# A shared centre tap between even and odd pixels in a Winograd-row convolution, with named buffers, a masked group norm and a re-planned order, on one Trainium2 core

## The chip, the core and the metric

The kernel runs on one core of one Trainium2 chip. The metric is device time in microseconds (us): the median of several runs of the same program. All tensors are float32, and TensorE takes each float32 matmul as two passes.

## The reference

The input x is (4 images, 128 channels, 128 x 128 pixels). Two layers follow, each with a residual.

```python
# layer 0
x = x + L0(group_norm(x))
# L0: block(v) + block(v transposed in space) transposed back, equal here to 2 * block(v)
# block, per pixel ("token") over 128 channels:
t = ln(t); y1 = ln(t)
t = t + (sigmoid(y1) * y1) @ W_out.T
y2 = ln(t); wht = y2 @ W_whiten.T
k = relu(wht @ W_key.T) ** 2                  # 512 wide
t = t + sigmoid(wht @ W_recep.T) * (k @ W_value.T)
# layer 1
x = x + L1(group_norm(x))
# L1: a 3x3 convolution (128 to 128 channels, padding 1) plus bias, times a squeeze-excite gate per channel
```

group_norm has 32 groups of 4 channels. The convolution needs the statistics of the whole image after layer 0, so an image is convolved only when its first layer is finished.

## The kernel before, in words

*Tiling.* Channels lie on the 128 partitions. An image is 32 chunks of 512 pixels (CH); two chunks make a group g (16 groups an image, 64 in all), and 16 image rows make a block k (8 an image, 32 in all), which is four chunks.

*Layer 0* (`layer0(g)`). For both chunks h of a group: the input is normalised on ScalarE (`u`, L757), turned to tokens-on-partitions on VectorE (`ut`, L886), has its statistics taken (`bn0`, L770), is scaled on ScalarE (`t`, L839) and multiplied and shifted by the norm's parameters (`g`, `b`, L908 and L911, on GpSimd from group 2 on). Second norm (`bn1`, `z`), back to channels (by TensorE, `Tz` L942, or from group 22 on by DMA through `zd`, `zs`, `zc`), silu, the attention product (`att`, L954), the residual (`T`, L959), third norm (`bn2`, whose factor goes through `four`, `rrow`, `rd`, `R`). t goes back to channels by DMA too (`td` L850, `ts`, `tt`). `cp` (L1015) makes y2. Then four key products `pk` (L1033), a relu each on ScalarE (L1038), a square each (on ScalarE L1044, or on VectorE L1050, as the table `SQUARES` says), the receptance `pr` (L1058), four value products `kv` (L1071) that accumulate into one bank, the gate step `q` (L1080) that reads that bank, the residual add on GpSimd (`x1`, L1086) and the statistics of the result (`bx`, L1094). A finished block is stored to DRAM (`xo`, L1101).

*Layer 1* (`conv(k, at)`). Rows are combined so that six products give four output rows (a Winograd transform along the rows): VectorE makes v1, v2, v3, v4, v0, v5 (L1179 to L1193) from rows of the block; TensorE makes m_i from v_i (`product`); VectorE and ScalarE combine the m_i into four rows (L1218 to L1239), and the block is stored (L1249). Each v_i and m_i is 128 x 512: four rows of 128 pixels. A product is three matmuls into one bank, one for each tap along the row; the outer taps leave out one column at the edge of the image:

```python
nc.tensor.matmul(pc, u[:, 1], vv, start=True, stop=False)
nc.tensor.matmul(pc[:, :, 1:W], u[:, 0], vv[:, :, 0 : W - 1], start=False, stop=False)
nc.tensor.matmul(pc[:, :, 0 : W - 1], u[:, 2], vv[:, :, 1:W], start=False, stop=True)
```

*Weights.* `conv_setup(b, at)` makes the second group norm and the gate of image b (`cag`, `cpm`, `csp`, ... `csg`) and scales the six transformed weights uw (`us` L621, `ut2` L627). `input_norm(b, at)` makes the first group norm of image b: the channel means of `bn_aggr` are averaged over the four channels of a group by one-column matmuls on TensorE (L498, L500), the variances by more of them, then GpSimd takes the root.

*What sets the order.* Nothing is left to the hardware's choice. `Plan` records every step with its engine, an assumed cost, a priority (its group, plus an entry of the table `SHIFT`), what it reads and writes and what buffers it takes; `Plan.order` lists the steps by simulated start on five in-order engines (TensorE, VectorE, ScalarE, GpSimd, and SyncE, whose queue issues the DMAs), and the kernel emits the instructions in that order. `ROOM` says how many buffers each kind has, also the eight PSUM banks: 3 of `Bh` (pk, pr, small products), 1 of `Bkv`, 2 of `Btr` (att and the TensorE transposes), 2 of `Bconv` (m_i). Buffers of a kind are taken in rotation. The convolution of image b is given priorities from group 16(b+1)+2 on, two groups apart for each block, so that it runs beside layer 0 of image b+1; the last image's convolution has nothing beside it. While the head of the kernel has gaps on TensorE, matmuls of no use (`fill`, L411) keep it going.

Of the kernel before, what the change touches and what calls it, by code (L numbers as in the profile page):

```python
# [13 lines left out]
P = 128  # L14
# [9 lines left out]
    "R": -94.694, "Rc": 15.085, "Rm": -2.646, "S": 24.009, "T": -84.8, "Tz": -36.19, "W": -22.14,  # L24
    "ab": 37.315, "att": 1.644, "b": 31.731, "bn0": 11.794, "bn1": -17.35, "bn2": -15.592,
    "bx": 49.609, "c": 7.82, "cag": 6.719, "cav": -18.068, "cd": -103.804, "cp": -37.768,
    "cp1": -27.368, "cpm": -17.233, "cpr": -71.755, "cpv": -65.194, "cre": 48.407, "crt": -73.005,
    "csg": -26.086, "csp": -39.311, "cth": -29.247, "cve": 53.942, "e": 12.136, "e0": 14.7,
    "e1": -70.81, "e2": -55.971, "edge": 60.492, "fw": 14.887, "g": -16.106, "gag": -13.379,
    "gnb": -14.148, "gpm": -2.701, "gpv": -23.531, "grt": -1.635, "gsp": -6.989, "gve": -30.013,  # L30
    "hot": -13.329, "in": 26.361, "in0": 105.375, "kv": 3.816, "late": 12.753, "m0": 23.5,
    "m1": -101.213, "o": -54.585, "pk": 3.497, "pq": -18.954, "pr": 3.288, "q": -106.007,
    "raw": -61.508, "rc": -6.337, "re": -93.796, "silu": -97.676, "sq": -115.033, "sqd": -34.912,
    "t": -2.49, "tD": -49.255, "tR": 16.588, "tW": -20.948, "th": -60.823, "tt": 105.266,
    "u": 16.271, "us": -19.465, "ut": 67.807, "ut2": 9.337, "uw": -50.513, "v": 57.985, "w": 117.982,
    "w0": 44.736, "w1": -43.048, "w2": -6.943, "x": 70.181, "x1": -70.076, "xc": 6.78, "xd": 2.407,
    "xf": -58.371, "xo": -10.863, "xs": -54.606, "y": 24.867, "z": 15.121, "zD": 21.243,
    "zR": 18.813, "zW": -13.966,
}
SQUARES = (("DDAA", "DDAA"), ("AAAA", "AAAA"))  # L40
# [3 lines left out]
LOOK = {'PE': 0.018, 'DVE': 0.087, 'ACT': 0.048, 'POOL': 0.004, 'SP': 0.048}  # L44
HASTE = 31.975
SQUARES_AT = 17
ROOM = dict(
    x=3, xd=2, xs=2, ut=3, t=7, z=2, y=2, zd=2, zc=2, td=2, tt=2, R=2, y2=2, h=6, r=2, xc=2, vt=3, v=4,
# [3 lines left out]
BACKLOG = 1.96  # L52
FIRST_U_ON_DVE = (2, 3)


XF_BUS, FIRST_XD, LATE_AT = 3.4, -25, -5
FILL_UNTIL, FILL_STEP = 330, 1.2
FIRST_FILL = {6: 3, 7: 2}
# [29 lines left out]

class Plan:
# [11 lines left out]
    def op(self, name, eng, cost, prio, emit, reads=(), writes=(), new=(), port=False, bus=0.0):  # L101
# [13 lines left out]
        for u in (*reads, *writes):  # L115
            if u[0] in self.users:
# [3 lines left out]
                 new=[t for t, _ in new], port=port, bus=bus)  # L120
# [3 lines left out]
    def order(self):  # L124
# [14 lines left out]
        freed, queue, taken = {}, {}, {}  # L139
# [12 lines left out]
        def slots(o):  # L152
            at = 0.0
            count = {}
            for t in o["new"]:
                tag = self.home[t]
                k = taken.get(tag, 0) + count.get(tag, 0)
                count[tag] = count.get(tag, 0) + 1
                if k >= self.room[tag]:
                    old = queue[tag][k - self.room[tag]] if k - self.room[tag] < len(queue[tag]) else None  # L160
                    if old is None or pending[old]:
                        return INF
                    at = max(at, freed[old])
            return at

        while done < n:
# [54 lines left out]
            for t in o["new"]:  # L221
                tag = self.home[t]
                queue.setdefault(tag, []).append(t)
                taken[tag] = taken.get(tag, 0) + 1
            for t in touches[i]:
                pending[t] -= 1
                freed[t] = max(freed.get(t, 0.0), en)
            for j in after[i]:
                reach = (self.OWN if ops[j]["eng"] == e else self.REACH)[ops[j]["eng"]]
                ready[j] = max(ready[j], en + reach)  # L230
                left[j] -= 1
                if not left[j]:
                    waiting[ops[j]["eng"]].append(j)
# [9 lines left out]
def conv_preact_kernel(  # L243
# [42 lines left out]
        z=[P, SUB, C], y=[P, CH], y2=[P, CH], h=[P, CH], r=[P, CH],  # L286
        xc=[P, BLK_ROWS + 2, W], vt=[P, Q, W], v=[P, Q, W], yt=[P, Q, W], uw=[P, 3, P],
# [9 lines left out]
    def make(t, tag):  # L297
        pool = ps if tag[0] == "B" else sb
        T[t] = pool.tile(SHAPE[tag], F32, tag=tag, name=t[0], bufs=ROOM[tag])
        return T[t]  # L300

    def bank(name):
        return ps.tile([P, CH], F32, tag="Bh", name=name, bufs=ROOM["Bh"])

    def staged(name, n, src=None):
        t = sb.tile([P, n], F32, tag="h", name=name, bufs=ROOM["h"])
# [4 lines left out]
    vec = sb.tile([5, C], F32, tag="vt", name="vec", bufs=ROOM["vt"])  # L311
# [3 lines left out]
    for name, src in (("g0row", ln0_g), ("b0row", ln0_b)):  # L315
        row0.append(sb.tile([1, C], F32, tag="y2", name=name, bufs=ROOM["y2"]))
# [3 lines left out]
    wo = sb.tile([P, P], F32, tag="v", name="wo", bufs=ROOM["v"])  # L320
# [26 lines left out]
    gmat = gmat.rearrange("p a b -> p (a b)")  # L347
    gturn = const.tile([P, SUB, P], F32, tag="gturn", name="gturn")
    for q in range(SUB):
# [3 lines left out]
        )  # L353

# [10 lines left out]
    ones = sb.tile([1, P], F32, tag="r", name="ones", bufs=ROOM["r"])  # L365
    nc.gpsimd.memset(ones, 1.0)

    warm = sb.tile([P, 1], F32, tag="r", name="warm", bufs=ROOM["r"])
# [38 lines left out]
    fill = ps.tile([P, CH], F32, tag="Bconv", name="fill", bufs=ROOM["Bconv"])  # L407
# [14 lines left out]
    READ, WRITE = (0, 0.85), (0, 0.4)  # L422

    def op(name, eng, cost, prio, emit, reads=(), writes=(), new=(), port=False, bus=0.0):
        return plan.op(name, eng, cost, prio + SHIFT.get(name, 0.0), emit, reads, writes, new, port, bus)
# [58 lines left out]
    def input_norm(b, at):  # L484
# [5 lines left out]

        def aggregate():
            S["mv"] = col("mv0", 2)
            nc.vector.bn_aggr(S["mv"], st0.pop(b).rearrange("p n s -> p (n s)"))

        def grouped(key, src, own):
            pm = T[key]
            for q in range(SUB):
                nc.tensor.matmul(pm[:, q : q + 1], gturn[:, q], src, start=True, stop=True)  # L498
            if own:
                nc.tensor.matmul(pm[:, SUB : SUB + 1], gmat, src, start=True, stop=True)  # L500

        def means():
            make(("pm0", b), "Bh")
            grouped(("pm0", b), S["mv"][:, 0:1], True)

        def spread():
# [5 lines left out]
            S["q"] = q  # L512

        def variances():
            make(("pv0", b), "Bh")
            grouped(("pv0", b), S["q"], False)
# [13 lines left out]
        step("gag", V, (0.4, 0.5), aggregate, [(s, i) for i in range(NCH)], [(("gnv", b), 0)])  # L530
        step("gpm", E, (0.5, 0.55), means, (), [(("pm0", b), 0)], [(("pm0", b), "Bh")])
        step("gsp", V, (0.65, 0.75), spread, [(("pm0", b), 0)])
        step("gpv", E, (0.4, 0.45), variances, (), [(("pv0", b), 0)], [(("pv0", b), "Bh")])
# [4 lines left out]
    def conv_setup(b, at):  # L538
# [7 lines left out]
        def small(name, eng, cost, fn, bank=None):  # L546
            t = (name, b)
            step(name, eng, cost, fn, (), [(t, 0)] if bank else (), [(t, "Bh")] if bank else ())
# [58 lines left out]
        small("csp", V, (0.8, 0.9), spread)  # L607
        small("cpv", E, (0.1, 0.15), variances, True)
        small("cve", V, TINY, with_eps)
# [3 lines left out]
        small("cre", V, (0.2, 0.3), rect)  # L613
        small("cpr", E, (0.3, 0.35), second, True)
        small("cth", A, (0.6, 0.75), tanh)
# [13 lines left out]
        for i in (1, 2, 3, 4, 0, 5):  # L629
# [10 lines left out]
            )  # L640
            if i in TAP:
                op("ut2", V, (0.21, 0.29), at, lambda i=i: tapped(i), [(t, 0)], [(t, 0)], (), True)

# [677 lines left out]
```

## Time and profile before

| what | us |
|---|---|
| median of 3 runs | 1744.41 (1743.2 to 1745.63) |
| the profiled execution | 1742.63 |
| its span, first to last instruction | 1740.9 |
| first key product (pk) starts | 71.1 |
| products of the convolution of images 0, 1, 2, 3 begin | 428.9, 850.0, 1301.5, 1612.4 |
| last value product (kv) | 1578.2 |
| last matmul | 1736.4 |
| m products on PE (L1203, L1204, L1205) | 197.7 + 195.4 + 194.9 busy |

A line of instruction groups gives the line of the kernel, engine, operation, tiles out<-in, shapes and count, then the busy time in us and the mean duration in ns, then the engine's idle time just before them and what ended it. A busy time is a union, so overlapping matmuls count once, and the durations of matmuls are longer than the spacing of their starts, since they are pipelined. PEld is TensorE's weight load. The granted TensorE clock was 0.997 on average.

### The profile page before, as it was taken

To read this page: it belongs to the slowest core of one execution; us is meant where nothing else is said; L and a number is where in the kernel's file an instruction comes from. 1 tells how busy PE (TensorE), PEld (TensorE's weight loads), DVE (VectorE), ACT (ScalarE), POOL (GpSimd) and SP (SyncE) were. 2 spreads that over 40 slices of the span, in tenths; PEclk is the share of its full clock that TensorE was granted. 3 is DMA by queue.
4 is the path that set the end of the run, shared out by engine and by line. 5 is a ranking of instruction groups with operands and counts; after the bars stand their busy time and mean duration, and the time that the engine had idled before them with its cause. 6 is when DMAs were issued, how large, how long until landed. Compare 5 with 4: busy or idle time off the path is not lost.

```text
span 1740.9 us, 18709 instructions
## 1 busy us (share of the span) xinstructions
PE 1690.7 (97%) x4872; PEld 815.7 (47%) x4872; DVE 1424.9 (82%) x2619; ACT 1293.8 (74%) x2656; POOL 1184.0 (68%) x1085
## 2 busy tenths in 40 slices
PE   5899999999999999999999999999999999999999
PEld 2444544444444445444445445454544444444443
DVE  5898888788889967798998887888897766448986
ACT  1999998898988887889889877998887875440000
POOL 1778887788987885879777886988878773310000
PEclk9999999999999999999999999999999999999999
DMA  9366675466577777578778877577776565215321
GB/s 326 91 213 202 193 219 194 145 206 230 153 250 246 252 230 236 199 232 247 250 245 245 254 238 240 178 218 236 241 254 199 183 204 176 101 75 224 154 98 73
DMA packets 140170, 354.66 MB, mean 204 GB/s; under 512 B 19079, under 2 KB 78750, under 8 KB 122782
## 3 DMA queue, kind: packets, MB, share of 16 engines
q1 hardware_dynamic: 139472, 352.99, 63.1%
q8 instruction: 39, 0.64, 0.2%
q14 instruction: 69, 0.57, 0.1%
q10 hardware_dynamic: 590, 0.46, 0.1%
HBM read 230.31 MB, written 123.07 MB: 203 GB/s over the span
## 4 chain that ended last, share of the span: by engine, by line
PE 71%; ACT 10%; POOL 8%; DVE 7%; DMA 2%; issue 2%; SPq 0%; ACTq 0%; DVEq 0%; POOLq 0%
PE kv L1071 19%; PE pk L1033 18%; PE m L1203 7%; PE m L1204 7%; PE m L1205 7%; PE att L954 5%; PE pr L1058 5%; ACT t L839 2%; ACT h L1038 2%; POOL rs L820 2%; ACT z L839 2%; DVE st L770 1%; ACT h L1044 1%; POOL x L1026 1%; POOL t L908 1%
## 5 line engine op out<-in xcount | busy, mean ns | idle before, releaser
L1071 PE MATMUL kv<-h,wv 128*128 128x512 f32 x1024 | 525.8, 598 | 4.6 <-DVE r L1080 2.6
L1033 PE MATMUL pk<-y,wk_s 128*128 128x512 f32 x1024 | 480.9, 595 | 4.7 <-ACT h L1038 3.1
L1038 ACT ACTIVATE h<-pk,kbias 128x512 f32<-128x512 f32 x512 | 336.1, 682 | 90.9 <-PE pk L1033 88.3
L1033 PEld LDWEIGHTS pk<-y,wk_s 128*128 128x128 f32 x1024 | 190.0, 190 | 239.3 <-issue 178.1
L1071 PEld LDWEIGHTS kv<-h,wv 128*128 128x128 f32 x1024 | 183.0, 190 | 205.3 <-issue 164.1
L1044 ACT ACTIVATE h<-h 128x512 f32<-128x512 f32 x444 | 267.5, 629 | 2.6
L1086 POOL TENSOR_TENSOR x<-x,r 128x512 f32<-128x512 f32 x128 | 169.8, 1327 | 132.0 <-DVE r L1080 128.5
L820 POOL TENSOR_TENSOR rs<-rs,nhalf 128x8 f32<-128x8 f32 (+1 forms) x134 | 227.2, 1700 | 47.3 <-ACT rs L817 45.1
L839 ACT ACTIVATE z<-t,nb,rs 128x128 f32<-128x128 f32 x512 | 208.7, 489 | 21.8 <-POOL nb L825 20.9
L839 ACT ACTIVATE t<-ut,nb,rs 128x128 f32<-128x128 f32 x512 | 209.7, 488 | 8.5 <-POOL nb L825 4.8
L908 POOL TENSOR_TENSOR t<-t,g 128x512 f32<-128x512 f32 x124 | 161.2, 1301 | 68.0 <-ACT t L839 67.6
L770 DVE BATCH_NORM_STATS2 st<-t 128x6 f32<-128x256 f32 x512 | 187.1, 410 | 22.9 <-POOL t L911 22.7
L1203 PE MATMUL m<-v,uw 128*128 128x512 f32 x384 | 197.7, 596 | 3.9 <-DVE v L1182 3.9
L1204 PE MATMUL m<-v,uw 128*128 128x508 f32 x384 | 195.4, 590 | 0.0
L1205 PE MATMUL m<-v,uw 128*128 128x508 f32 x384 | 194.9, 589 | 0.0
L1015 POOL TENSOR_TENSOR y<-tt,R 128x512 f32<-128x512 f32 x96 | 130.9, 1367 | 59.8 <-PE pk L1033 46.9
L1026 POOL TENSOR_TENSOR x<-tt,x 128x512 f32<-128x512 f32 x124 | 162.5, 1324 | 3.9 <-DMA tt<-ts 3.7
L911 POOL TENSOR_TENSOR t<-t,b 128x512 f32<-128x512 f32 x124 | 162.7, 1319 | 2.6
L954 PEld LDWEIGHTS att<-wo,y 128*128 128x128 f32 x1024 | 130.9, 192 | 51.7 <-issue 33.1
L1063 ACT ACTIVATE r<-pr,rbias 128x512 f32<-128x512 f32 x128 | 87.1, 681 | 72.6 <-PE pr L1058 36.2
L1058 PE MATMUL pr<-y,wr_s 128*128 128x512 f32 x256 | 132.3, 600 | 3.9 <-ACT h L1038 3.0
L954 PE MATMUL att<-wo,y 128*128 128x128 f32 x1024 | 132.8, 276 | 0.4 <-ACT y L947 0.3
(160 smaller groups left out, 2278.6 us busy)
## 6 DMA issues: line engine op xcount, KB each, us to landing
xd<-in_x SPq DMA_DIRECT2D x128, 256.0 KB
x<-in_x SPq DMA_DIRECT2D x32, 1024.0 KB
xo<-x SPq DMA_DIRECT2D x32, 1024.0 KB
R<-rd SPq DMA_DIRECT2D x63, 512.0 KB
ts<-td SPq DMA_DIRECT2D x248, 128.0 KB
tt<-ts SPq DMA_DIRECT2D x62, 512.0 KB
out<-xc SPq DMA_DIRECT2D x31, 1024.0 KB
xc<-xo SPq DMA_DIRECT2D x24, 1152.0 KB
```

Of the source, the lines that this page charges most:

```text
L770: nc.vector.bn_stats(st[:, i : i + 2, :].rearrange("p n f -> p (n f)"), two)
L820: nc.gpsimd.tensor_tensor(T[rs][:, part], T[rs][:, part], nhalf[:, :k], ALU.pow)
L839: nc.scalar.activation(dst[:, s, :], src[:, s, :], AF.Identity, bias=nb[:, i : i + 1], scale=rs[:, i : i + 1])
L954: nc.tensor.matmul(pa[:, ts(m, P)], T[y][:, ts(m, P)], wo2, start=True, stop=True)
L1033: nc.tensor.matmul(make(pk, "Bh"), wk_s[:, ts(j, P)], T[y2], start=True, stop=True)
L1038: nc.scalar.activation(make(hh, "h"), T[pk], AF.Relu, bias=kbias[:, j : j + 1])
L1044: nc.scalar.activation(T[hh], T[hh], AF.Square)
L1058: nc.tensor.matmul(make(pr, "Bh"), wr_s, T[y2], start=True, stop=True)
L1071: nc.tensor.matmul(T[kv], wv[:, j, :], T["h", g, h, j], start=(j == 0), stop=(j == NH - 1))
L1203: nc.tensor.matmul(pc, u[:, 1], vv, start=True, stop=False)
L1204: nc.tensor.matmul(pc[:, :, 1:W], u[:, 0], vv[:, :, 0 : W - 1], start=False, stop=False)
L1205: nc.tensor.matmul(pc[:, :, 0 : W - 1], u[:, 2], vv[:, :, 1:W], start=False, stop=True)
```

## The change

1. *Shared centre tap.* For blocks k < 24 (images 0 to 2) the products 1, 3, 0 and 5 are made otherwise (`PARITY`). v_i is written as two runs, the even pixels of the rows and the odd ones. With taps a, c, b (left, centre, right) and pair k of even and odd pixels e and o, the even output pixel is c(e[k] + o[k]) + (b - c)o[k] + a o[k-1], and the odd one c(e[k] + o[k]) + (a - c)e[k] + b e[k+1]: both hold the centre tap of the sum. VectorE makes that sum (`su`, 256 columns) and once an image the differences of outer and centre taps (`ud`); TensorE makes four products of 256, 252, 256 and 252 columns into the bank of m_i and one shared product of 256 columns (`cm`) into a bank of `Btr`; VectorE adds the shared bank to what is made of m_i (`cs`, 512 columns).
2. *Squares.* The tile h holds two chunks' worth of hidden units (1024 columns), three of them in place of six; most squares are taken on ScalarE over 1024 columns at once ("W").
3. *Buffers.* A buffer of a kind is taken by name, whichever was freed first, and not in rotation. `zd` and `td` have one buffer each, where they had two.
4. *Masked first norm.* Means and variances are multiplied by a 0/1 mask (`own`) on VectorE, and one matmul of four columns with `gany` takes the place of four of one column.
5. *Order.* All entries of `SHIFT` and other planner settings are new; the first four groups have entries for each half (`lag`). The planner also knows of four waits in `conv_setup` that it left out before. The fill matmuls on the input in the head (`FIRST_FILL`) are gone.

Products 2 and 4, and all six in image 3, keep their three matmuls. The core of the diff:

```diff
-SQUARES = (("DDAA", "DDAA"), ("AAAA", "AAAA"))
+SQUARES = (("DAWW", "DDWW"), ("WWWW", "WWWW"))
+SUM_BANK = "Btr"
...
-    x=3, xd=2, xs=2, ut=3, t=7, z=2, y=2, zd=2, zc=2, td=2, tt=2, R=2, y2=2, h=6, r=2, xc=2, vt=3, v=4,
+    s=2, ud=4,
+    x=3, xd=2, xs=2, ut=3, t=7, z=2, y=2, zd=1, zc=2, td=1, tt=2, R=2, y2=2, h=3, r=2, xc=2, vt=3, v=4,
...
-FIRST_FILL = {6: 3, 7: 2}
+FIRST_FILL = {}
...
+def PARITY(k):
+    return (0, 1, 3, 5) if k < 24 else ()
...
-        T[t] = pool.tile(SHAPE[tag], F32, tag=tag, name=t[0], bufs=ROOM[tag])
+        T[t] = pool.tile(SHAPE[tag], F32, tag=f"{tag}-{plan.slot[t]}", name=t[0], bufs=1)
...
+        def split(name, src):
+            S[name] = col(name, SUB)
+            nc.vector.tensor_scalar(S[name], own, src, None, ALU.mult)
...
-            grouped(("pm0", b), S["mv"][:, 0:1], True)
+            nc.tensor.matmul(pm[:, :SUB], gany, S["m4"], start=True, stop=True)
+            nc.tensor.matmul(pm[:, SUB : SUB + 1], gmat, S["mv"][:, 0:1], start=True, stop=True)
...
+                    nc.vector.tensor_tensor(make(ud, "ud"), u[:, 0::2], u[:, 1:2].to_broadcast([P, 2, P]), ALU.subtract)
...
+                elif how == "W" and not first:
+                    def square(hh=hh):
+                        x = T[hh].rearrange("p a b -> p (a b)")
+                        nc.scalar.activation(x, x, AF.Square)
...
+                def both(i=i, su=su):
+                    x = flat_halves(i)
+                    dst = make(su, "s").rearrange("p (q k) -> p q k", q=Q)
+                    nc.vector.tensor_tensor(dst, x[:, 0], x[:, 1], ALU.add)
...
+                    nc.tensor.matmul(pc[:, 0], d[:, 1], x[:, 1], start=True, stop=False)
+                    nc.tensor.matmul(pc[:, 0, :, 1:], u[:, 0], x[:, 1, :, : W // 2 - 1], start=False, stop=True)
+                    nc.tensor.matmul(pc[:, 1], d[:, 0], x[:, 0], start=True, stop=False)
+                    nc.tensor.matmul(pc[:, 1, :, : W // 2 - 1], u[:, 2], x[:, 0, :, 1:], start=False, stop=True)
...
+                    nc.tensor.matmul(make(mm, SUM_BANK)[:, : CH // 2], T["uw", b, i][:, 1], T[su], start=True, stop=True)
...
+                t = by_parity(get(n))
+                row = T[name_of(f"mm{i}")][:, : CH // 2].rearrange("p (q k o) -> p q k o", q=Q, o=1)
+                tt(t, row.to_broadcast([P, Q, W // 2, 2]), t, ALU.add)
```

## The prediction

> **What bounds the kernel now.** I read the page's totals and its chain of waits first, then the busy time of each engine in stretches of the span, then who TensorE waits for, then single matmuls in time order.
>
> ```profile
> PE 1690.7 (97%) x4872; PEld 815.7 (47%) x4872; DVE 1424.9 (82%) x2619; ACT 1293.8 (74%) x2656; POOL 1184.0 (68%) x1085
> ...
> PE 71%; ACT 10%; POOL 8%; DVE 7%; DMA 2%; issue 2%; SPq 0%; ACTq 0%; DVEq 0%; POOLq 0%
> ```
>
> A busy PE need not be a full one, so the stretches decide (length, then the busy time of PE, PEld, DVE, ACT, POOL):
>
> ```profile
> 0.00:80.00 80.00, 53.70 (x181) 29.71 (x182) 55.11 (x111) 43.05 (x105) 33.40 (x63) 0.98 0.70 220
> 80.00:330.00 250.00, 239.86 (x790) 120.86 (x789) 214.10 (x414) 229.53 (x479) 201.35 (x192) 0.99 0.62 196
> 330.00:600.00 270.00, 266.13 (x799) 129.96 (x798) 238.39 (x454) 236.10 (x496) 228.67 (x208) 1.00 0.69 214
> 600.00:1370.00 770.00, 767.85 (x2199) 370.09 (x2198) 650.62 (x1192) 657.71 (x1342) 626.23 (x548) 1.00 0.73 230
> ...
> 1580.00:1612.00 32.00, 28.49 (x74) 12.57 (x72) 29.80 (x61) 2.09 (x5) 1.47 (x2) 1.00 0.70 271
> 1612.00:1741.00 129.00, 124.63 (x288) 55.21 (x288) 106.76 (x175) 10.20 (x16) 0.00 (x0) 0.99 0.28 110
> ```
>
> From 600 to 1370 us PE lacks 2.2 us in 770. DVE is busy for 650.6, 84.5% of it. The waits of PE in that stretch name almost nothing:
>
> ```profile
> PE kv L1071 <- DVE r L1080: 0.9, 2, 0.8
> PE cpv L565 <- DVE q L561: 0.5, 1, 0.5
> PE pr L1058 <- POOL y L1015: 0.5, 1, 0.5
> PE pk L1033 <- ACT h L1038: 0.2, 1, 0.2
> ```
>
> Are the matmuls back to back? The timeline gives starts, and each x2 is the two passes of one fp32 matmul:
>
> ```profile
> 704.45 1.02 PE L1203 MATMUL m<-v,uw 128*128 128x512 f32 x2
> 705.31 1.01 PE L1204 MATMUL m<-v,uw 128*128 128x508 f32 x2
> 706.16 1.01 PE L1205 MATMUL m<-v,uw 128*128 128x508 f32 x2
> 707.01 1.02 PE L1071 MATMUL kv<-h,wv 128*128 128x512 f32 x2
> ...
> 784.66 1.02 PE L1071 MATMUL kv<-h,wv 128*128 128x512 f32 x2
> 785.52 1.05 PE L954 MATMUL att<-wo,y 128*128 128x128 f32 x8
> ```
>
> A product of three matmuls starts at 704.45 and its successor at 707.01: 2.56 us. The steady spacing in the trace is 0.4295 us a pass for 512 columns, 0.426 for 508 and 0.1115 for 128 (0.112 for one column). So the convolution costs TensorE its columns, and while images 0 to 2 are convolved beside the next image's first layer, every column taken away is time.
>
> **The products: minus 40.0 us.** Four of six products (1, 3, 0, 5) in 24 of 32 blocks change: 96 of 192. Before, two passes each of 512, 508 and 508 columns: 2 x (0.4295 + 2 x 0.426) = 2.563 us. After, two passes each of 256, 252, 256, 252 and the shared 256. No 256-column row exists. Half of the 512 row gives 0.2148 us, the line between the 128 and 512 rows 0.2175; I take 0.216 (0.2125 for 252): 2 x (3 x 0.216 + 2 x 0.2125) = 2.146. Saved 0.417 each, x96 = 40.0 us; the two ends give 41.1 and 38.5.
>
> One rule would cancel this. The Trainium skill, "TensorE: Matmul & The Clock Gate", section "The mechanism", lets a weight load overlap running matmuls only in another row group, and "LDWEIGHTS (loading the stationary operand)" prices 128 columns at about 107 ns. All these matmuls use all rows. With loads exposed, ten passes in place of six would add 4 x 0.107 = 0.43 us and turn the saving into a loss of about 1 us over 96 products. The rows say otherwise: a 512-column pass with its own load takes 0.4295 us, and a 128-column pass, again with its own load, 0.1115: little more than the page gives the load alone. At 256 columns there is twice that room. I stay with 40.0.
>
> **The masked first norm: minus 5.0 us.** Each image's group means took 18 one-column passes and now take 6 (two of four columns and one of one): 12 x 0.112 = 1.34 us. For images 1 to 3 this lies on the full PE, 4.0 us; in the head it is on the chain before the first image, where two masking steps on DVE (0.16 each, as L520) come in: 1.0 us net.
>
> **The order in the head: 0, between -8 and +8.** In the built order of before, pr, four pk and four kv of group 0 (0.86 + 3.4 + 3.4 us) stand among the groups' att and transposes and have run by 80 us. In the order of after all these att and transposes come first, then nine fill matmuls (7.7 us of warming), then the first pk. That can cost the 7.7 us. What it feeds is a stretch (80 to 330) that lost 10.1 us on PE, with ACT at 92%. With a stock of finished inputs some of these come back. I put it at nought. ACT stays as tight there: squares become 51 on DVE (68 before), 17 single and 222 double on ACT (444 single before).
>
> **What is added, all on DVE: plus 84 us of work, of which I charge 12.** In 96 products a sum of the two halves (256 elements; nearest row L770, 256 elements, 0.33 us start to start) and an addition of the shared bank (512, one PSUM input, nearest L1222 to L1239, 0.60 to 0.63 from start to start where DVE doesn't idle): 96 x 0.94 = 90. Twelve tap differences at 0.33 = 4, eight masks 1, less 17 squares at 0.67 = 11. Sum 84. The strided forms read two runs in turn; L770 reads its two rows the same way at full rate, so I add nothing for the stride (0 to 5 us).
>
> It fits beside PE only just. From the gate product of group 24 to that of group 56, before takes 768 us (601 to 1369). Counting instructions in the built orders at the rates above, PE has 754 us before and 772 after (18 blocks of products there, 15 before), DVE 578 and 686. Measured, DVE was busy 649, a factor 1.12. In the dense piece 487 to 601 us DVE was busy 104.5 of 114.2 us for a counted 97.7, a factor 1.07, and PE still 113.0. So after: DVE 733 (1.07) to 769 (1.12) in a stretch where PE needs 772. The factor is mostly this (DVE busy of L1189, first with GpSimd working, then with it idle):
>
> ```profile
> 600.00:1370.00 770.00, 15.45 (x14) 1.00 0.73 230
> 1612.00:1741.00 129.00, 5.46 (x8) 0.99 0.28 110
> ```
>
> 1.10 us against 0.68: a DVE step with two SBUF inputs waits for a GpSimd step. The half sums and the tap differences are of that kind (up to 0.2 us more each, 108 x 0.2 = 22 of the 84 us again); the additions of the shared bank, one input in PSUM, are not. Behind a late DVE stand the gate step (frees the only kv bank, the next kv waits in PE's queue), t plus att, and v. At 91% busy (487 to 601) PE lost 1.2 us in 114, 1%; at 95% I take 1.5% of 772 us. Cover all gone: 30 us or more.
>
> **Edits at nought.** Double squares on ACT: 222 start later than single ones by one relu (0.57 us by L1038), hidden by other PE work, since PE's queue mixes pk and kv of different groups; at the last group, where nothing else is left to mix in, it costs one such relu at most. Buffers named by who is free first: no instruction. td and zd with one buffer: the transposes at 703.3 are written by transfers issued from 704.0 to 710.7 and fetched at 714.2, and the next come about 24 us later (768 / 32); if that failed, DVE's queue would stop behind the transpose, 0 to 5 us. The shared product uses the two banks of att and the transposes; att waits in PE's queue if both are held, 0 to 5 us. Stage change to image 3: 13.5 us of products are left behind the last kv in place of 28.2, but the chain from there to image 3's first product was itself held up by those products; its PE stall was about 5 us (28.5 busy of 32, and slower matmuls for a moment after it) and I leave it.
>
> **Sum.** 1740.9 (span) - 40.0 - 5.0 + 0 + 12 = 1707.9. The profiled execution took 1742.6 and the median is 1744.4, 3.5 over the span: 1711.
>
> **Rivals.** (1) *DVE shares the bound*: 733 becomes 769 and PE stalls 4 to 5% in the conv stretches: 15 to 25 us more, 1726 to 1736, middle 1730. For it: 84.5% plus 84 us; against: only 2.2 us of stall now, and 91% did no harm. (2) *DVE is the bound, slower*: half sums at L1189's hindered price (0.53), factor 1.12 and a DVE that cannot be over 94% busy because it too waits: 769 / 0.94 = 818 us for the stretch, 46 over PE's 772. It gives back the whole 45 saved, with some in the stretch before: 1750. It decides from a DVE share of about 97% of PE's need. (3) *The weight loads are not hidden at 256 columns*: no gain from products, 1711 + 41 = 1752; the 128-column row excludes nearly all of it. (4) *The new order also removes stalls*: half of the 14 us lost between 80 and 600 and of the 5 at the stage change come back and DVE costs nothing: 1711 - 10 - 12 = 1689.
>
> **How the numbers follow.** Main case, 1700 to 1720: 0.58. Rival 1: 0.22. Rivals 2 and 3: 0.08 and 0.01. Rival 4: 0.11. Within 0.2% (3.5 us, about what a measurement of this kernel can tell from no change) falls 0.03 of rival 1 and 0.02 of rival 2. Faster 0.58 + 0.19 + 0.11 = 0.88, same 0.05, slower 0.07. The range takes in the main case, most of rival 1 and half of rival 4: 1694 to 1738.
>
> **What would show it.** PE's 256-column passes spaced 0.216 us; 96 shared products of 0.43 us; DVE busy near 1500 us. In a stretch like 600 to 1370 PE still over 98% busy, with "kv waits for the gate step" and "m waits for v" a few us and not tens. First pk near 80 us, then fewer stalls until 330. I am wrong if PE falls to 95% in the conv stretches with DVE over 95%, if passes of 256 columns are spaced 0.3 us, or if the head's late start is not made good.

## The result, and the profile after

| | before | after |
|---|---|---|
| median of 4 runs each, us | 1743.81 (1740.49 to 1745.63) | 1723.65 (1722.64 to 1728.7) |
| ratio | | 0.9892, 95% interval 0.9868 to 0.9917 |
| profiled execution, us | 1742.63 | 1728.7 |
| its span, us | 1740.9 | 1727.0 |

The change makes the kernel about 20 us (1.1%) faster. Forecast were 33. The profiled execution of after is the longest of its four runs; the other three lie between 1722.64 and 1723.97, so its head is read below together with those of the experiments.

The totals and the chain of the page after:

```profile
PE 1654.8 (96%) x5212; PEld 881.8 (51%) x5212; DVE 1491.0 (86%) x2814; ACT 1283.8 (74%) x2451; POOL 1182.2 (68%) x1091
...
PE 63%; DVE 13%; POOL 9%; ACT 6%; DMA 4%; issue 4%; SPq 0%; ACTq 0%; POOLq 0%; DVEq 0%
```

VectorE stands at 13% of the chain that ended last, where before it had 7%. The stretches (length, then busy PE, PEld, DVE, ACT, POOL):

```profile
0.00:80.00 80.00, 44.38 (x145) 24.90 (x146) 52.81 (x108) 40.46 (x100) 32.46 (x65) 0.98 0.80 230
80.00:330.00 250.00, 243.90 (x815) 125.77 (x814) 210.18 (x421) 236.66 (x480) 212.45 (x202) 0.99 0.64 191
...
600.00:1350.00 750.00, 741.98 (x2400) 408.15 (x2398) 703.63 (x1329) 618.98 (x1164) 597.85 (x525) 1.00 0.74 234
1350.00:1560.00 210.00, 208.49 (x634) 111.79 (x635) 140.12 (x250) 133.07 (x217) 108.16 (x90) 1.00 0.46 152
1560.00:1600.00 40.00, 27.72 (x96) 17.98 (x95) 37.41 (x74) 1.64 (x5) 2.72 (x3) 0.86 0.64 245
```

From 600 to 1350 us PE lacks 8.0 us in 750 (before 2.2 in the same 750) and DVE is at 93.8%. From 1560 to 1600, the change to image 3, PE is busy for 27.7 of 40 us, and DVE for 37.4. The matmuls themselves, by their starts:

```profile
706.60 1.02 PE L1146 MATMUL kv<-h,wv 128*128 128x512 f32 x2
707.46 0.59 PE L1331 MATMUL m<-v,ud 128*128 128x256 f32 x2
707.89 0.59 PE L1332 MATMUL m<-v,uw 128*128 128x252 f32 x2
708.31 0.59 PE L1333 MATMUL m<-v,ud 128*128 128x256 f32 x2
708.75 0.59 PE L1334 MATMUL m<-v,uw 128*128 128x252 f32 x2
709.17 0.59 PE L1337 MATMUL mm<-s,uw 128*128 128x256 f32 x2
709.60 1.02 PE L1146 MATMUL kv<-h,wv 128*128 128x512 f32 x2
```

A product with its shared tap goes from 707.46 to 709.60: 2.14 us, as forecast (2.146).

**A ledger of TensorE.** For each matmul pass take the distance from its start to the next start. Its steady value is read from the traces for each width (0.4295 us for 512 columns, 0.426 for 508, 0.216 for 256, 0.2125 for 252, 0.1115 for 128); call that *need*. What a distance has beyond it is *lost*; fill matmuls count as lost too. The head ends with the first product of image 0, the convolution stretch with the last value product, and the rest is the stage change and image 3. Each column is one profiled execution.

| us | before | after | difference |
|---|---|---|---|
| need | 1633.9 | 1588.5 | -45.4 |
| lost in the head (start to 428.9; to 439.8) | 77.5 | 80.7 | +3.2 |
| lost in the convolution stretch (to 1578.6; to 1569.5) | 12.7 | 30.9 | +18.2 |
| lost at the stage change and after | 6.0 | 16.0 | +10.0 |
| sum | | | -14.0 |

That is the difference of the two spans (13.9). Half of the 30.9 us lies in gaps of 0.05 to 0.25 us between matmuls that overlap in the records, which a busy time does not show: PE passes the forecast's mark of 98% (742 of 750 us) and loses all the same. The work that left TensorE is what was forecast (45.0), to half a microsecond; the error is in what TensorE loses. Who it waits for in the convolution stretch is scattered; the profile names a dozen waits, the longest 2.1 us:

```profile
PE pk L1088 <- POOL y L1070: 2.1, 1, 2.1
PE pk L1088 <- ACT h L1094: 1.7, 3, 0.8
PE kv L1146 <- DVE r L1155: 1.6, 4, 1.1
PE mm L1337 <- DVE e L1360: 1.5, 1, 1.5
```

At the stage change two waits hold 11.5 of the 16.0 us (total, count, longest):

```profile
PE cp L613 <- DVE avg L610: 6.9, 1, 6.9
PE m L1347 <- DVE uw L661: 4.6, 1, 4.6
```

Another 2.6 us are matmuls at a lower clock behind these waits. The granted clock was 0.50 from 1590 to 1600 us, and the first product of image 3 took 5.11 us where 2.56 is usual:

```profile
1597.37 2.05 PE L1347 MATMUL m<-v,uw 128*128 128x512 f32 x2 [4.61 <-DVE uw L661]
...
1602.48 1.02 PE L1347 MATMUL m<-v,uw 128*128 128x512 f32 x2
```

Before has 2.0 us of the same kind at this place (granted clock 0.68 from 1610 to 1615 us).

### The profile page after: what moved, and what is told of

Its sections match the earlier page's. It is cut to its first block, busy times and chain, and to the rows that moved or that the text cites. A ratio compares the mean times of both kernels' runs of the same rounds, so it can differ in the third digit from the quotient of the medians.

```text
span 1727.0 us, 19571 instructions
## 1 busy us (share of the span) xinstructions
PE 1654.8 (96%) x5212; PEld 881.8 (51%) x5212; DVE 1491.0 (86%) x2814; ACT 1283.8 (74%) x2451; POOL 1182.2 (68%) x1091
## 4 chain that ended last, share of the span: by engine, by line
PE 63%; DVE 13%; POOL 9%; ACT 6%; DMA 4%; issue 4%; SPq 0%; ACTq 0%; POOLq 0%; DVEq 0%
PE kv L1146 17%; PE pk L1088 17%; PE pr L1133 5%; PE att L1006 4%; PE m L1347 4%; PE m L1348 4%; PE m L1349 4%; POOL rs L868 2%; DVE st L816 2%; POOL four L838 2%; PE mm L1337 2%; ACT z L887 2%; PE m L1331 1%; PE m L1333 1%; PE m L1334 1%
## 5 line engine op out<-in xcount | busy, mean ns | idle before, releaser
L1088 PE MATMUL pk<-y,wk_s 128*128 128x512 f32 x1024 | 498.7, 597 | 4.4 <-POOL y L1070 2.1
L1094 ACT ACTIVATE h<-pk,kbias 128x512 f32<-128x512 f32 x512 | 342.1, 681 | 90.9 <-PE pk L1088 60.7
L868 POOL TENSOR_TENSOR rs<-rs,nhalf 128x8 f32<-128x8 f32 (+1 forms) x134 | 231.2, 1729 | 37.4 <-ACT rs L865 36.3
L1113 ACT ACTIVATE h<-h 128x1024 f32<-128x1024 f32 x222 | 234.1, 1054 | 2.1
L887 ACT ACTIVATE t<-ut,nb,rs 128x128 f32<-128x128 f32 x512 | 209.6, 487 | 31.4 <-DVE st L816 22.6
L816 DVE BATCH_NORM_STATS2 st<-t 128x6 f32<-128x256 f32 x512 | 187.3, 412 | 13.3 <-POOL t L961 13.0
L838 POOL TENSOR_TENSOR four<-four,nhalf 128x8 f32<-128x8 f32 x63 | 110.5, 1755 | 41.9 <-ACT four L834 40.7
L1155 DVE SCALAR_TENSOR_TENSOR r<-r,kv 128x512 f32<-128x512 f32 x128 | 86.6, 677 | 48.7 <-PE kv L1146 47.1
L801 ACT ACTIVATE xd<-xd,nb,rs 128x512 f32<-128x512 f32 x126 | 97.1, 810 | 16.1 <-DMA xd<-in_x 12.7
L1138 ACT ACTIVATE r<-pr,rbias 128x512 f32<-128x512 f32 x128 | 86.9, 682 | 26.1 <-PE pr L1133 25.6
```

The costliest lines, as they stand in the source:

```text
L816: nc.vector.bn_stats(st[:, i : i + 2, :].rearrange("p n f -> p (n f)"), two)
L868: nc.gpsimd.tensor_tensor(T[rs][:, part], T[rs][:, part], nhalf[:, :k], ALU.pow)
L887: nc.scalar.activation(dst[:, s, :], src[:, s, :], AF.Identity, bias=nb[:, i : i + 1], scale=rs[:, i : i + 1])
L1088: nc.tensor.matmul(make(pk, "Bh"), wk_s[:, ts(j, P)], T[y2], start=True, stop=True)
L1094: nc.scalar.activation(dst[:, j % 2], T[pk], AF.Relu, bias=kbias[:, j : j + 1])
L1113: nc.scalar.activation(x, x, AF.Square)
```

## The experiments

*Theory at the start:* VectorE's added work makes the loss in the convolution stretch, and the order of VectorE's queue makes the stage change. *Rival:* the new order (with its buffers and double squares) makes both, or, at the stage change, VectorE's amount of work whatever the order. All runs were taken beside runs of the kernel before, whose medians in the three sets were 1743.77, 1744.23 and 1743.95. "Same order" means that every engine's list of instructions is that of after but for the edit. The losses are those of the ledger.

| run | median (range) us | ratio to before, 95% | need | lost: head, convolution, rest |
|---|---|---|---|---|
| before | 1743.81 | | 1633.9 | 77.5, 12.7, 6.0 |
| after | 1723.65 (1722.64 to 1728.7) | 0.9868 to 0.9917 | 1588.5 | 80.7, 30.9, 16.0 |
| e1 chain first | 1722.84 (1721.14 to 1723.71) | 0.9868 to 0.9909 | 1588.5 | 78.5, 30.2, 13.1 |
| e2 no half sums and additions | 1717.56 (1715.37 to 1720.12) | 0.9838 to 0.9881 | 1588.5 | 75.5, 25.6, 14.2 |
| e3 three matmuls | 1757.42 (1752.93 to 1760.99) | 1.0068 to 1.0113 | 1628.5 | 76.1, 26.4, 12.7 |
| e4 norm on before | 1741.88 (1738.24 to 1744.36) | 0.9974 to 1.0004 | 1628.5 | 77.2, 16.1, 7.5 |
| e5 last block plain | 1722.08 (1720.79 to 1723.73) | 0.9845 to 0.9891 | 1590.1 | 76.5, 31.5, 10.6 |
| e6 e1 and e5 together | 1722.32 (1717.19 to 1723.73) | 0.9840 to 0.9885 | 1590.1 | 78.6, 32.6, 8.9 |
| e7 old settings | 1848.22 (1846.64 to 1851.67) | 1.0570 to 1.0614 | 1588.5 | 98.8, 138.7, 12.2 |
| e8 single squares | 1726.48 (1722.18 to 1731.34) | 0.9871 to 0.9915 | 1588.5 | 78.2, 32.4, 15.0 |
| e9 no double squares | 1723.96 (1719.08 to 1729.13) | 0.9862 to 0.9901 | 1588.5 | 81.3, 30.7, 16.4 |
| e10 e2 and e9 together | 1714.39 (1714.34 to 1715.11) | 0.9818 to 0.9845 | 1588.5 | 74.1, 24.8, 14.4 |
| e11 no shared additions | 1720.66 (1717.13 to 1724.53) | 0.9850 to 0.9883 | 1588.5 | 78.2, 26.9, 13.5 |
| e12 two blocks plain, chain first | 1721.29 (1720.56 to 1722.94) | 0.9856 to 0.9886 | 1591.8 | 76.8, 31.2, 8.8 |

Up to the first product the steps of e1, e2, e3, e5, e6, e11 and e12 are those of after (but for the tap differences in e3), and the loss in the head is 75.5 to 80.7 us. So 5 us of it come and go between runs, and differences below 2 us in a median are not read.

**e1: the chain to image 3's weights first.**

```diff
+        rush = -1000 if b == B - 1 else 0
...
-            op(name, eng, cost, at, fn, [(c, 0), *reads], [(c, 0), *writes], new)
+            op(name, eng, cost, at + rush, fn, [(c, 0), *reads], [(c, 0), *writes], new)
```

and likewise for the scalings `us` and, right behind each, `ut2`.

> The kernel after (1723.65), with one change of order: at the change to image 3 the VectorE steps that make the gate and the weights of image 3 (variance, excitation, scaling of the weights) stand ahead of the leftover convolution steps of image 2, and the first product's weight is finished before the other weights are scaled. No instruction is added or removed; nothing differs before the last 150 us. Theory (TensorE stands idle 6.9 us at the stage change because the small step that reads the variance has 13 leftover steps ahead of it in VectorE's queue, and 4.6 us more because six scalings stand before the first finished weight): 8 to 10 us come back, about 1714. Rival (the leftover products end at the same time whatever the order, and their combining steps, now later, hold the first rows or the banks of image 3): 0 to 3 us, about 1722.

Measured: 1722.84. In the trace the stage change loses 13.1 in place of 16.0. VectorE's queue of after, by start and duration, shows why so much was expected: `rs<-cpv` needs only a matmul that ended at 1583.7.

```profile
1582.33 0.68 DVE L1392 SCALAR_TENSOR_TENSOR xc<-e,e 128x512 f32<-128x512 f32 x1
...
1589.53 0.68 DVE L1286 TENSOR_TENSOR v<-xc 128x512 f32<-128x512 f32 x1
1590.13 0.15 DVE L603 TENSOR_SCALAR rs<-cpv 128x1 f32<-128x1 f32 x1
...
1593.56 3.26 DVE L655 SCALAR_TENSOR_TENSOR uw<-uw,rs,row 128x384 f32<-128x384 f32 x6
1596.74 0.89 DVE L661 SCALAR_TENSOR_TENSOR uw<-ident,uw 128x128 f32<-128x128 f32 x4
1597.55 0.74 DVE L1288 SCALAR_TENSOR_TENSOR v<-p,mg,q 128x512 f32<-128x512 f32 x1
```

In e1 the matmul ends at 1580.9 and the step runs at 1581.00. PE's waits in the same stretch of e1:

```profile
PE m L1349 <- DVE v L1290: 7.6, 1, 7.6
PE cp L615 <- DVE avg L612: 1.6, 1, 1.6
PE cpr L625 <- DVE a L619: 0.6, 1, 0.6
```

The wait for `avg` shrank from 6.9 to 1.6 and that for `uw` went, and a wait of 7.6 us for the first v of image 3 (L1288 in after) came in their place: that v stands behind all that the chain was moved past. VectorE has no pause from 1569 to 1595 in e1, and 2.4 us of pauses in after (all behind `rs<-cpv`, from 1590.3 on). The expectation of the fifth run calls that no pause at all; it is nearly so. The rival holds: what VectorE has to do between the last value product and the first product of image 3 takes nearly the same time in either order. From the end of the last value product to that first product it is 27.8 us in after and 25.0 in e1, and VectorE is busy for 25.3 and 25.1 of them.

**e2: no half sums, no additions.** The steps `su` and `cs` are left out, and the shared product streams a constant, so the output is not the convolution.

```diff
-                    nc.vector.tensor_tensor(dst, x[:, 0], x[:, 1], ALU.add)
+                    pass
...
-                tt(t, row.to_broadcast([P, Q, W // 2, 2]), t, ALU.add)
+                pass
```

> The kernel after, same order, with 192 VectorE steps left out: the half sums (su) and the additions of the shared bank (cs). The shared product streams a constant in place of the sum, so TensorE has the same matmuls; the output is not the convolution. About 90 us of VectorE work go. Theory (VectorE's load causes the 20 us that TensorE loses more than before between 400 and 1550 us, since it is busy 94% there): 12 to 18 us faster, 1706 to 1712, nearly all between 400 and 1550 us. Rival (the loss is made by the new order, the fewer buffers or the shared banks): 0 to 4 us, 1720 to 1724.

Measured: 1717.56, 6.1 us faster, between theory and rival: half of the 12 that were the least expected. DVE's busy time fell from 1491.0 to 1402.9 (88 us, as counted), and from 600 to 1350 us to 649.05, 86.5%:

```profile
600.00:1350.00 750.00, 744.21 (x2398) 410.33 (x2397) 649.05 (x1215) 623.79 (x1172) 602.54 (x526) 1.00 0.75 235
```

Yet PE lacks 5.8 us there, of the 8.0 in after, and the convolution stretch loses 25.6 in place of 30.9. VectorE's new work explains 5 of the 18 us, not all, and 1.8 of the 10 at the stage change (14.2 in place of 16.0).

**e3: the old three matmuls in the new order.** The products 1, 3, 0, 5 are three matmuls of 512, 508 and 508 columns again (they read the two runs as if these were rows, so the outer taps meet other pixels: the output is not the convolution), and `su`, `cs`, `ud` and the shared product are left out.

```diff
-                    nc.tensor.matmul(pc[:, 0], d[:, 1], x[:, 1], start=True, stop=False)
-                    nc.tensor.matmul(pc[:, 0, :, 1:], u[:, 0], x[:, 1, :, : W // 2 - 1], start=False, stop=True)
...
+                    nc.tensor.matmul(pw, u[:, 1], x, start=True, stop=False)
+                    nc.tensor.matmul(pw[:, :, 1:W], u[:, 0], x[:, :, 0 : W - 1], start=False, stop=False)
+                    nc.tensor.matmul(pw[:, :, 0 : W - 1], u[:, 2], x[:, :, 1:W], start=False, stop=True)
```

> The kernel after, same order of all other steps, with products 1, 3, 0, 5 made by three matmuls of 512, 508 and 508 columns again, no half sums, no additions, no tap differences. TensorE has 40 us more work, VectorE 94 us less. Theory: the shared tap is worth its 40 us less the VectorE stall of 12 to 18 us, so this takes 1723.65 + 40 - 15 = 1749 (1744 to 1752), which is no better than the kernel before: order, buffers and squares together are worth nothing. Rival (the gain of the change is from order, buffers, squares and norm, and the products are worth little): 1725 to 1735.

Measured: 1757.42, slower than before by 0.7 to 1.1% and above both expectations (the theory ended at 1752). The products are worth 33.8 us (1757.42 - 1723.65); 40 less the 6.1 of e2 are 33.9. And e3 loses 26.4 us in the convolution stretch without one step of the new VectorE work.

**e4: the masked norm alone, on before.** The lines of change 4, nothing else.

```diff
-            grouped(("pm0", b), S["mv"][:, 0:1], True)
+            pm = make(("pm0", b), "Bh")
+            nc.tensor.matmul(pm[:, :SUB], gany, S["m4"], start=True, stop=True)
+            nc.tensor.matmul(pm[:, SUB : SUB + 1], gmat, S["mv"][:, 0:1], start=True, stop=True)
```

> The kernel before with the masked first norm alone; every other step in the same order. TensorE has 48 one-column matmuls less (12 an image, 0.112 us each, of 5.4 us in all), VectorE eight steps of about 0.16 us more. Theory (TensorE is the bound between 430 and 1580 us, so what leaves it there leaves the time): 4 to 6 us faster, about 1739. Rival (the norm's matmuls lie in gaps that TensorE has anyway, or the two extra steps delay its chain): 0 to 1 us, about 1743.

Measured: 1741.88, 12 runs: 1.9 us less than before, with an interval that touches nought. The need fell by 5.4 as counted; 4.6 us of other losses stand against it in the trace (3.4 of them in the convolution stretch), so the result lies between theory and rival. e3 and e4 have the same need, 1628.5, and the same function in TensorE; they differ by the order, the buffers and the squares: 15.5 us in the medians. The ledger has 10.3 us of it in the convolution stretch and 5.2 at the stage change, with 1.1 less in the head. They also differ in how VectorE writes v and reads m (even and odd pixels apart), but that made VectorE no busier: 1394.3 us in all in e3 (with 17 squares fewer), 1428.6 in e4.

**e5, e6, e12: fewer shared taps at the stage change.** In e5 `PARITY` ends at block 23 in place of 24; e6 adds the edit of e1; e12 is e6 with an end at 22.

```diff
-    return (0, 1, 3, 5) if k < 24 else ()
+    return (0, 1, 3, 5) if k < 23 else ()
```

> The kernel after (1723.65), with the last block of image 2 made by three matmuls a product (the shared tap for 23 blocks in place of 24); the order is the same until that block. TensorE gets 4 x 0.417 = 1.7 us more work, VectorE loses 4 half sums and 4 additions, 3.7 us, all at the change to image 3, where the trace of after shows VectorE busy without a pause from the last value product to the first product of image 3. Theory (VectorE's work sets the stage change, so the order of its steps mattered little): 2 to 4 us faster than after, 1720 to 1722. Rival (the chain through the gate of image 3, or TensorE's own work, sets it): 0 to 2 us slower, 1724 to 1726.

> Both edits at the stage change: the chain to image 3's weights first in VectorE's queue (as in the first experiment, 1722.84) and the last block of image 2 by three matmuls a product. Theory (VectorE's work sets the stage change; the order alone moved the wait from the gate to the first v of image 3): the 3.7 us of VectorE work come off that wait, 1718 to 1721. Rival: as the first experiment plus 1.7 us of TensorE work, 1723 to 1725.

> Both edits at the stage change, with the last two blocks of image 2 by three matmuls a product in place of one (the shared tap for 22 blocks). One block brought TensorE's loss at the stage change from 13.4 us to 6.8 in the trace, for 1.7 us more of products; the median moved by 1.3. Theory (VectorE's work there still sets it): the second block's 3.7 us take 2 to 3 us more of the loss and cost 1.7 us, 1720 to 1722. Rival (what is left is the start of TensorE after idling and the last chain): 1.7 us slower than with one block, 1723 to 1725.

Measured: 1722.08 (the upper end of the theory), 1722.32 (between theory and rival) and 1721.29 (inside the theory). The loss at the stage change goes from 16.0 to 10.6, 8.9 and 8.8, for 1.6, 1.6 and 3.3 us more need: a net gain in the traces of 3.8, 5.5 and 3.9. On the same count e1, which only moves steps, gains 2.9. In the medians it is 1.6, 1.3 and 2.4 (0.8 for e1), within the spread of the runs, so these four runs do not rank less work above a better place.

Nor is the comparison clean. The planner orders what follows the edit anew: in e5 `avg` starts at 1578.44, ahead of ten combining and v steps, where in after it stood behind such steps. The nearest pair is e1 and e6, both with the chain first. VectorE is busy for 25.1 us in e1 and 21.7 in e6 between the last value product and image 3's first product, and that stretch is 25.0 and 23.8 us: 3.4 us less work made it 1.2 us shorter. Most of the rest of the smaller loss is that TensorE has 15.4 us of products to do there in place of 13.3. What remains in e12 is the first v of image 3 again, at the end of VectorE's line, and 2.9 us of slow matmuls at the start of image 3, which is a part of what the rival named:

```profile
PE m L1349 <- DVE v L1290: 6.0, 1, 6.0
```

e12 has the lowest median of the runs that leave no step out (1.3% below before). Its interval overlaps that of after, so that it beats after is likely and not shown.

**e7: the old settings with the new work.**

```diff
-LOOK = {'PE': 0, 'DVE': 0, 'ACT': 0.102, 'POOL': 0.088, 'SP': 0}
-HASTE = 50.979
+LOOK = {'PE': 0.018, 'DVE': 0.087, 'ACT': 0.048, 'POOL': 0.004, 'SP': 0.048}
+HASTE = 31.975
```

with `BACKLOG` and all entries of `SHIFT` that before has.

> The kernel after with the planner's settings of before (all entries of SHIFT that before has, LOOK, HASTE, BACKLOG; no entries for the halves of the first groups), so in another order; products, squares, buffers and norm as in after. Theory (between 440 and 1570 us TensorE loses 31 us where before lost 13, and 26 of them even with the old products in the new order, so the new order made them; the old settings bring them and the stage change back): 1708 to 1716. Rival (the old settings do not suit the new VectorE work, or the loss comes with the double squares and the buffers): 1724 to 1740.

Measured: 1848.22; theory and rival both miss by over 100 us. The work is that of after, and TensorE loses 138.7 us in the convolution stretch:

```profile
PE pr L1115 <- POOL y L1052: 24.6, 6, 10.2
PE m L1313 <- DVE v L1270: 23.9, 7, 6.2
```

The settings of before don't suit the new steps, so this run does not tell what the new order costs; it tells that the new work under the old settings is 104 us slower than before.

**e8, e9: the double squares.** e8 makes each as two of 512 columns at the same place; e9 leaves them out, so that layer 0 is another function.

```diff
-                        x = T[hh].rearrange("p a b -> p (a b)")
-                        nc.scalar.activation(x, x, AF.Square)
+                        for half in range(2):
+                            x = T[hh][:, half]
+                            nc.scalar.activation(x, x, AF.Square)
```

> The kernel after, same order, with each double square on ScalarE (1024 columns) made as two of 512 columns at the same place: ScalarE has some 20 us more work. Theory of the prediction (double squares cost nothing and ScalarE is not the bound after 400 us): 0 to 4 us slower, 1723 to 1727, if anything in the head, where ScalarE is busy 94%. Rival (the late end of a double square is what makes the key products wait): 3 to 6 us faster, 1718 to 1721.

> The kernel after, same order, with the 222 double squares on ScalarE left out (the value products take the unsquared units, so layer 0 is another function): some 210 us of ScalarE work go, TensorE's matmuls stay. It asks what makes the key and receptance products wait between 440 and 1570 us (TensorE loses 31 us there, 26 without the half sums). Theory (ScalarE: its squares delay the relu that frees the bank of the next key product): 6 to 10 us come back there, and up to 6 in the stretch from 80 to 330 us where ScalarE is busy 94%: 1708 to 1716. Rival (ScalarE is not it; the waits come from the chain of dependences in this order): 0 to 3 us, 1720 to 1724.

Measured: 1726.48 and 1723.96. Splitting costs 0 to 3 us, as the theory had it. The squares themselves are busy for 254.4 us in place of 234.1, the 20 more that were counted; ScalarE's total, in which instructions that overlap count once, grows by 11.7. Without double squares ScalarE loses 195 us of its 1284 (from 600 to 1350 us it is busy 513 in place of 619) and TensorE loses as much as ever:

```profile
600.00:1350.00 750.00, 740.29 (x2397) 408.27 (x2396) 707.20 (x1329) 512.98 (x1043) 594.87 (x524) 1.00 0.75 233
```

The rival of e9 holds. ScalarE's squares are not what holds TensorE up, though "pk waits for ACT h" is among the longest waits, and being 95% busy between 80 and 330 us (87% in e9) costs nothing either (13.4 us lost from the first pk to the first product, 11.5 in after).

**e10: no double squares, no sums, no additions.** The edits of e2 and e9 together.

> The kernel after, same order, without the double squares and without the half sums and shared additions (both as in the single experiments): neither ScalarE nor VectorE can be short any more. Theory (the loads of the two engines make most of TensorE's loss between 440 and 1570 us): it falls from 31 us to under 15, the time to 1700 to 1708. Rival (most of that loss is dependence and order): it stays above 20 us, 1712 to 1717.

Measured: 1714.39. With DVE at 87% and ACT at 69% in the same stretch, PE still lacks 7.6 us of 750:

```profile
600.00:1350.00 750.00, 742.37 (x2396) 410.93 (x2395) 653.99 (x1211) 514.77 (x1047) 599.06 (x526) 1.00 0.75 234
```

The convolution stretch loses 24.8, so the rival holds: most of that loss is not the load of these two engines. That it is how the steps depend on each other in this order is what is left, and is argued: the waits stay scattered, the longest 1.8 us and for GpSimd's `y`, and no run takes work from GpSimd or the DMAs.

**e11: half sums kept, additions left out** (the output lacks the centre tap).

```diff
-                tt(t, row.to_broadcast([P, Q, W // 2, 2]), t, ALU.add)
+                pass
```

> The kernel after, same order, with the 96 additions of the shared bank left out and the half sums kept (the output lacks the centre tap). VectorE has about 58 us less work, and the shared product's bank is free when TensorE has written it. Theory (of the 6 us that sums and additions cost together, the hold of the bank until the addition is the larger part: the shared product waits 5.6 us for VectorE in the trace of after, 0.3 us without sums and additions): 4 to 6 us faster, 1718 to 1720. Rival (the half sums, which have two inputs in SBUF and meet GpSimd there, are the larger part): 0 to 2 us, 1722 to 1724.

Measured: 1720.66, 3.0 us faster, between the two theories; the additions and the half sums share the 6.1 us about evenly, as far as the spread of the runs can tell. The ledger's distances ahead of a shared product lose 5.6 us in after and 0.3 in e2.

## Why the prediction was nearly right

The forecast of 33 us and the 20 measured, as the runs split them:

| term | forecast | measured | by |
|---|---|---|---|
| products on TensorE | -40.0 | -40.0 | need of e3 against after: 1628.5 - 1588.5 |
| VectorE's added work | +12 | +6.1 | e2 against after |
| masked norm | -5.0 | -1.9 (-4.5 to +0.7) | e4 against before |
| order, buffers, squares | 0 | +15.5 | e3 against e4 |
| sum | -33 | -20.3 | measured in all: -20.2 |

The first two lines add up to -33.9; e3 against after measures them together at -33.8. That agreement is a test; the sum is none, since after against e3, e3 against e4 and e4 against before add up to the whole by their making.

The median of 1723.65 lies in the stated range (1694 to 1738), but 13 us above the point, outside the main case (1700 to 1720) and below rival 1 (1726 to 1736). That it is no further off is in part luck: 6 us too many were charged to VectorE, and they cover 6 of the 15.5 us that the new order brought. No rival had the new order as a cost; rival 4 had it as a gain.

- **The products, right.** The 256-column passes are spaced 0.216 us, the 252-column ones 0.2125. The weight loads stay hidden at 256 columns: five pairs of passes, each with its own load, take 2.14 us. The sentence of the Trainium skill, "TensorE: Matmul & The Clock Gate", section "The mechanism", on which the objection rested (a load overlaps running matmuls only where the row group differs) does not hold for these matmuls, at 256 columns as at 512. The same section also lets a load go ahead into a background weight buffer, which the prediction left out; no run here shows whether that is how these loads are hidden.
- **DVE's charge, too high.** The work came as counted (88 us for the half sums and additions, 90 forecast; busy 1491.0 us, near 1500). PE was forecast to lose by DVE's share, and DVE's share was as feared: 93.8%. But with 86.5% (e2) PE lost nearly as much, so the busy share, on which the 1.5% rested (91% busy, 1% lost), was a poor measure of the loss. The charge was also taken on 772 us alone, a part of the 1150 us (428.9 to 1578.2) in which convolution and layer 0 run together; over all of it the same 1.5% is 17 us. And rival 1's 4 to 5% of 772 us is 31 to 39, so 19 to 27 more than the 12, not 15 to 25.
- **The head, right.** First pk at 88.6 us (84 to 87 in the experiments with this order; forecast near 80), and from there to the first product 11.5 us lost where before lost 26.2. Together +3.2 us in this profile, -2 to +3 over the runs, against a forecast of 0, -8 to +8.
- **The step that failed: the order outside the head, and with it "stage change: I leave it".** The prediction priced the new order only in the head. In the convolution stretch and at the stage change it took the losses of before as given and put VectorE's charge on top. e3 and e4, with the same TensorE work, show 15.5 us between the two orders (with their buffers and squares), 10.3 and 5.2 us by the ledger in these two places. At the stage change the leftover products were cut from 28.2 to 13.5 us, and the text argued that the chain "was itself held up by those products". They were not the main thing that held it. With 15 us fewer of them (28.2 to 13.3 in the traces) the stretch from the last value product to image 3's first product shrank by 6 us only, from 33.8 to 27.8. VectorE is busy for 31.4 us of it in before and for 25.3 in after, and the leftover steps in its queue stand ahead of the chain (e1). Its amount of work is not all of it either: in e3, which has the order of after, VectorE is busy for 22.0 us and the stretch is still 27.5. Thus products that had covered VectorE's work are gone, and what is left uncovered shows as 16 us of loss in place of 6, the slow matmuls after it included.
- **The norm, too high.** That a full TensorE gives back each microsecond taken from it holds for the products. For 48 one-column matmuls the run does not show it: of their 5.4 us 1.9 arrived, and the interval of e4 (-4.5 to +0.7) holds both nought and most of it.
- **Edits at nought.** Double squares: nought (e8, e9). Single td and zd, named buffers: not tried apart. In the trace of after VectorE waits 0.4 us in all for `td` to be free and 0.2 for `zd`, so the single buffers stop it hardly at all; what they do to the order and the DMA queue is not shown. Shared product in the banks of att: att waits 0.8 us for its additions, and the shared product itself loses 5.6. Both waits are for VectorE's new steps, which cost 6.1 in all.

What stays open: which part of the order, the named buffers, the shared tile h and single td and zd makes the 14 to 15 us between e3 and e4. e3 has none of VectorE's new work, the double squares are excluded (e8, e9), and putting the old settings under the new work gave another, far slower schedule (e7).

## What to carry to other kernels

When a change takes work off the bound engine and also comes with a new order, price the order everywhere and not only where it looks different: the saving was exact, and the order, with the buffers that came with it, took back 15 us of it. A busy share of 94% and a name in the list of waits are no proof: leaving that engine's work out (195 us of ScalarE for no gain, 88 of VectorE for 6) says what it holds up. And where an engine hardly pauses during a stage change, moving its steps mostly moves the wait (e1). How much of its work the bound engine's leftover work covers is to be counted before that cover is cut.

## What the hardware showed beside

By groups of after (mean ns after the busy time):

```profile
L1316 DVE TENSOR_TENSOR s<-v 128x256 f32<-128x256 f32 x96 | 50.6, 530 | 0.3
...
L683 DVE TENSOR_TENSOR ud<-uw 128x256 f32<-128x256 f32 x12 | 8.1, 702 | 0.1
```

A half sum with both inputs in SBUF takes 0.53 us on average (the hindered price of rival 2) and 0.41 where GpSimd is idle, at the stage change. A tap difference of as many columns takes 0.70. A double square of 1024 columns takes 1.05 us, and two single ones 1.15 (e8's squares, 254.4 us over 222 pairs).
